# Two-cell recurrence on one core: the sum of the states and the forget products move from GpSimd to VectorE, with a new order of the steps

## The chip, the cores and the metric

The kernel runs on one core of a Trainium2 chip. The metric is the device time in microseconds of one launch, the median of several runs. All times below are microseconds unless marked ns.

A core has engines with a queue each, and each works through its queue in order: TensorE (PE in the profile: matmuls and transposes; its weight loads are listed as PEld), VectorE (DVE), ScalarE (ACT), GpSimd (POOL) and SyncE (SP, which here only issues DMAs). An instruction waits at the head of its queue until the semaphores that it names are high enough; everything behind it on that engine waits with it.

## What is computed

The input is one image of 256 x 256 positions with 32 channels. Four residual layers follow each other, each on the group norm of its input:

```python
x = x + gated_values(gn(x))      # layer 0
x = x + sobel(gn(x))             # layer 1
x = x + sobel(gn(x))             # layer 2
x = x + recurrence(gn(x))        # layer 3
```

The last one takes most of the time. It treats the 256 rows of the image as 256 sequences and the 256 columns as time steps; two cells (layers 0 and 1 of the recurrence) with 128 hidden values each are stacked:

```python
def step(carry, x_t):
    z = x_t @ W_lat + b_lat
    for j in range(2):
        zz = concatenate([z, h[j]]) @ W_cell[j] + b_cell[j]
        zz = group_norm(zz)                    # 4 groups: the 4 gates
        i, f, o, g = split(zz, 4)
        c[j] = sigmoid(f) * c[j] + sigmoid(i) * tanh(g)
        h[j] = sigmoid(o) * tanh(c[j])
        z = z + h[j]
    return x_t + z @ W_out + b_out
```

So a step of a cell needs its own state of the step before, cell 1 needs cell 0's new state too, and the output of a step needs the sum of both states, h[0] + h[1].

## The kernel before, in words

The first three layers take about 640. The recurrence (`recurrence`, from L720) keeps the image in SBUF. The 256 sequences are two halves of 128, one per partition. A step has four units, (layer, half): 00, 01, 10, 11. All of them go through the same operations, each named by a short word in the code:

- x: the product of the input with the folded input weights, for two units at once (`project`, L770); it begins the accumulation of a unit's 128x512 pre-activations `zz` in PSUM. i (L790): for cell 1, the product of cell 0's new state. m (L795): the product of the unit's own state of the step before; it closes `zz`. All three on TensorE.
- sq (L803): the squares of `zz`, on ScalarE. rd (L808): their sums per gate, `ve`, on VectorE. pw (L811): these to the power -0.5, `rs`, 128x4, on GpSimd. The means are zero because the weights were centred beforehand.
- si, sf, so, tg (L784): the four gates, on ScalarE, scaled by `rs`. The output gate has a tile of its own, `go`; the others share `ga`.
- ig (L832): input gate times candidate, VectorE. fc (L837): forget gate times old cell state; on GpSimd for cell 0, on VectorE for cell 1. c (L841): their sum, VectorE. th (L845): its tanh, ScalarE. h (L848): output gate times that, VectorE.
- T (L853): the transpose of h on TensorE into PSUM. e (L857): its copy to SBUF, `hT`, on VectorE; the matmuls i and m of what follows use it as weights.
- hs (`both`, L862): once a step the sum of both cells' `hT`, 128x256, on GpSimd.
- Once in four steps the output of a block of four columns (`emit`): o0 (L868) a matmul of the residual, o1 (L871) four matmuls on the four `hs`, of (L880) the bias on ScalarE, ot a transpose on VectorE and four DMAs on SP.

Nothing is left to a scheduler here. The order on each engine is written out by hand: the table `PLAN` gives each operation of each unit a time within a step of length `PERIOD`, `OUT` does it for the output, and the program adds t x PERIOD, sorts all entries of all 256 steps by that time and issues them in this order. The numbers thus only set the order; an instruction starts when its engine is free and its semaphores are met. Since a unit's operations spread over several periods, several steps are in flight: while cell 0 is at step t, cell 1 is some two steps behind, and `hs` follows later still.

`sums` and `roots` (the tiles of `ve` and `rs`) are rings with one slot for each of the last `SLOTS` steps. A slot that is used again waits for those that used it last.

The kernel has a second copy of the recurrence for norm weights that are not all one and zero; with these inputs it isn't run.

Of the kernel before, what the change touches and what calls it, by code (L numbers as in the profile page):

```python
# [17 lines left out]
T = 256  # L18
# [5 lines left out]
L = 2  # L24
# [633 lines left out]
class RecurrentInputs:  # L658
# [40 lines left out]

SLOTS = 64
PERIOD = 8.700
PLAN = {
    (0, 0): dict(m=3.34, sq=3.72, rd=4.73, pw=5.61, ga=5.84, sf=5.86, so=6.12, fc=6.24),
    (0, 1): dict(m=7.00, sq=7.12, rd=8.38, pw=8.64, ga=9.88, sf=9.90, si=10.02, tg=10.28),
    (1, 0): dict(x=13.81, i=17.21, m=17.59, sq=18.47, rd=19.23, pw=19.73, ga=21.35, sf=21.37),
    (1, 1): dict(x=20.62, i=21.50, m=22.38, sq=23.14, rd=24.02, pw=25.15, ga=25.26, sf=25.28),
}
PLAN[0, 0].update(tg=6.37, si=6.75, ig=7.38, c=8.01, th=8.26, h=8.76, T=9.02, e=10.40)  # L710
PLAN[0, 1].update(fc=10.65, so=11.16, ig=11.28, c=11.54, th=12.17, h=12.55, T=12.92, e=15.19)
PLAN[1, 0].update(so=21.75, si=22.00, tg=22.25, fc=22.63, ig=22.76, c=22.88, th=23.39, h=24.27)
PLAN[1, 0].update(T=24.90, e=25.03)
PLAN[1, 1].update(tg=26.54, si=26.67, so=26.79, ig=26.92, fc=27.05, c=27.55, th=28.31, h=28.81)
PLAN[1, 1].update(T=29.69, e=30.58, hs=34.23)

OUT = dict(o0=29.06, o1=54.28, of=55.29, ot=68.15)


def recurrence(tc, out, ident, weights, inputs, general):  # L720

    nc = tc.nc
# [22 lines left out]
    kp = ctx.enter_context(tc.tile_pool(name="norm", bufs=1))  # L745
    sums = kp.tile([P, 2 * L, SLOTS, 4], F32, name="ve")
    roots = kp.tile([P, 2 * L, SLOTS, 4], F32, name="rs")
    sp = ctx.enter_context(tc.tile_pool(name="state", bufs=2))
# [8 lines left out]
    v = {}  # L757
    todo = []

    def at(when, what, *args):  # L760
        todo.append((when, len(todo), what, args))

    def project(l, h, t):

        if t >= T:
            return
        zz = v["zz", l, h] = ps_zz.tile([P, 4 * H], F32, name=f"zz{l}{h}")
        rows = slice(l * X1, l * X1 + KX)
        x = inputs.of(t, rows, slice(h * P, (h + 1) * P))
        nc.tensor.matmul(zz, lhsT=x, rhs=fx[rows, l, :], start=True, stop=l == 0 and t == 0)  # L770

    def one(name, l, h, t):
        seqs = slice(h * P, (h + 1) * P)
        get = lambda k: v[k, l, h]
        gates = lambda x, g: x[:, g * H : (g + 1) * H]
        four = lambda x: x.rearrange("p (g m) -> p g m", g=4)

        def gate(g, func):

            x, scale = (get("zn"), 1.0) if general else (get("zz"), get("rs")[:, g : g + 1])  # L780
            if g == 2:
                v["go", l, h] = up.tile([P, H], F32, name="go", bufs=3)
            dst = get("go") if g == 2 else gates(get("ga"), g)
            nc.scalar.activation(dst, gates(x, g), func, scale=scale)  # L784

        if name == "x":
            project(0, 1 - h, t + 1 + h)
            project(1, h, t)
        elif name == "i":
            nc.tensor.matmul(  # L790
                get("zz"), lhsT=v["hT", 0, t][:, seqs], rhs=wc[:, l, 0, :], start=False, stop=t == 0
            )
        elif name == "m":
            if t:
                nc.tensor.matmul(  # L795
                    get("zz"),
                    lhsT=v["hT", l, t - 1][:, seqs],
                    rhs=wc[:, l, 1, :],
                    start=False,
                    stop=True,  # L800
                )
        elif name == "sq":
            nc.scalar.activation(  # L803
                sqs[l, h][:, :, 0:H], four(get("zz")), AF.Square, scale=float(H**-0.5)
            )
        elif name == "rd":
            ve = v["ve", l, h] = sums[:, 2 * l + h, t % SLOTS, :]
            nc.vector.tensor_reduce(ve, sqs[l, h], AX.X, ALU.add)  # L808
        elif name == "pw":
            rs = v["rs", l, h] = roots[:, 2 * l + h, t % SLOTS, :]  # L810
            nc.gpsimd.tensor_tensor(rs, get("ve"), inputs.mhalf, ALU.pow)  # L811
        elif name == "ga":
            v["ga", l, h] = up.tile([P, 4 * H], F32, name="ga")
            if not general:
                return
            zn = v["zn", l, h] = up.tile([P, 4 * H], F32, name="zn")
            for g in range(4):
                nc.vector.scalar_tensor_tensor(
                    gates(zn, g),
                    gates(get("zz"), g),  # L820
                    get("rs")[:, g : g + 1],
                    gates(gam[:, l, :], g),
                    ALU.mult,
                    ALU.mult,
                )
            nc.vector.tensor_add(zn, zn, bet[:, l, :])
        elif name in ("si", "sf", "so", "tg"):
            g = ("si", "sf", "so", "tg").index(name)
            gate(g, AF.Tanh if name == "tg" else AF.Sigmoid)
        elif name == "ig":  # L830
            c = v["cn", l, h] = sp.tile([P, H], F32, name=f"c{l}{h}")
            nc.vector.tensor_mul(c, gates(get("ga"), 0), gates(get("ga"), 3))  # L832
        elif name == "fc":
            if t:
                fc = v["fc", l, h] = up.tile([P, H], F32, name="fc")
                eng = nc.vector if l else nc.gpsimd
                eng.tensor_mul(fc, gates(get("ga"), 1), get("c"))  # L837
        elif name == "c":
            c = get("cn")
            if t:  # L840
                nc.vector.tensor_add(c, c, get("fc"))  # L841
            v["c", l, h] = c
        elif name == "th":
            th = v["th", l, h] = up.tile([P, H], F32, name="th")
            nc.scalar.activation(th, get("c"), AF.Tanh)  # L845
        elif name == "h":
            hh = v["h", l, h] = up.tile([P, H], F32, name="h")
            nc.vector.tensor_mul(hh, get("go"), get("th"))  # L848
        elif name == "hs":
            both(t)  # L850
        elif name == "T":
            pt = v["pt", l, h] = ps_h.tile([P, 4 * H], F32, name="pt")
            nc.tensor.transpose(pt[:, 0:P], get("h"), ident)  # L853
        elif name == "e":
            if h == 0:
                v["hT", l, t] = hp.tile([P, S], F32, name=f"hT{l}")
            nc.vector.tensor_copy(v["hT", l, t][:, seqs], get("pt")[:, 0:P])  # L857

    def both(t):

        hs = v["hs", t] = hp.tile([P, S], F32, name="hs")
        nc.gpsimd.tensor_add(hs, *[v.pop(("hT", l, t)) if l else v["hT", l, t] for l in range(L)])  # L862

    def emit(blk, part):

# [24 lines left out]
    for k in range(inputs.NX, NB // inputs.XT):  # L890
        at(((k - inputs.NX + 1) * inputs.XT * J + 2.0) * PERIOD, inputs.load, k)
    for h in range(2):
        at(-1e5, project, 0, h, 0)
    at(PLAN[1, 1]["x"] - PERIOD, project, 0, 0, 1)
    for t in range(T):
        for (l, h), ops in PLAN.items():
            for name, when in ops.items():
                at(t * PERIOD + when, one, name, l, h, t)
    for blk in range(NB):
        for part, when in OUT.items():  # L900
            at((blk * J + J - 1) * PERIOD + when, emit, blk, part)
    todo.sort(key=lambda e: e[:2])
# [45 lines left out]
```

## Time and profile before

| | |
|---|---|
| time, median of 3 runs | 2883.52 (2879.49 to 2886.28) |
| the profiled execution's own time | 2880.13 |
| its span | 2878.2 |
| mean granted TensorE clock | 0.982 |
| TensorE busy | 2776.8 (96%) |
| VectorE busy | 2401.1 (83%) |
| ScalarE busy | 2369.6 (82%) |
| GpSimd busy | 1722.2 (60%) |
| `hs` on GpSimd, 256 times, mean | 774 ns |
| `fc` on GpSimd, 510 times, mean | 455 ns |
| first and last start of `hs` | 669.5, 2868.4 |

The span runs from the first to the last instruction of the profiled execution; its time is a little longer. The busy time of an engine counts neither its waits nor the instructions that only steer. In a line for a group of instructions stand the source line, the engine, the operation, output and inputs with shapes, the count, then the busy time in total and the mean of one in ns, then the idle time of the engine ahead of them and what ended most of it. The chain of waits follows the work that ended last back to its start: a stretch that belongs to TensorE is one in which only faster or better fed TensorE work would help.

### The profile page before, as it was taken

To read this page: it belongs to the slowest core of one execution; us is meant where nothing else is said; L and a number is where in the kernel's file an instruction comes from. 1 tells how busy PE (TensorE), PEld (TensorE's weight loads), DVE (VectorE), ACT (ScalarE), POOL (GpSimd) and SP (SyncE) were. 2 spreads that over 40 slices of the span, in tenths; PEclk is the share of its full clock that TensorE was granted. 3 is DMA by queue.
4 is the path that set the end of the run, shared out by engine and by line. 5 is a ranking of instruction groups with operands and counts; after the bars stand their busy time and mean duration, and the time that the engine had idled before them with its cause. 6 is when DMAs were issued, how large, how long until landed. Compare 5 with 4: busy or idle time off the path is not lost.

```text
span 2878.2 us, 38258 instructions
## 1 busy us (share of the span) xinstructions
PE 2776.8 (96%) x9561; PEld 1034.1 (36%) x9561; DVE 2401.1 (83%) x6505; ACT 2369.6 (82%) x6961; POOL 1722.2 (60%) x2076
## 2 busy tenths in 40 slices
PE   7899898989999999999999999999999999999997
PEld 4433333333333333333333333333333333333332
DVE  6788797977888888888888888888888888888886
ACT  5477676758888888888888888888888888888886
POOL 2311374656666666666666666666666666666665
PEclk9899998989999999999999999999999999999999
DMA  3000000000000000000000000000000000000000
GB/s 133 1 1 1 16 1 1 1 22 8 12 12 12 13 13 12 12 12 11 12 12 12 12 12 12 12 13 15 12 14 13 13 12 12 13 12 12 5 4 9
DMA packets 94333, 38.37 MB, mean 13 GB/s; under 512 B 74852, under 2 KB 91269, under 8 KB 94104
## 3 DMA queue, kind: packets, MB, share of 16 engines
q1 hardware_dynamic: 93156, 34.67, 5.1%
q8 instruction: 81, 1.33, 0.2%
q14 instruction: 148, 1.21, 0.1%
q10 hardware_dynamic: 148, 0.86, 0.1%
q0 software_dynamic: 800, 0.30, 0.0%
HBM read 10.63 MB, written 8.39 MB: 7 GB/s over the span
## 4 chain that ended last, share of the span: by engine, by line
PE 76%; DVE 9%; POOL 7%; ACT 5%; issue 1%; DVEq 0%; POOLq 0%; ACTq 0%
PE zz L795 26%; PE zz L770 15%; PE zz L790 11%; PE pt L853 5%; POOL rs L811 4%; PE pv L279 4%; PE pg L452 4%; DVE c L841 4%; PE pg L412 3%; DVE ve L808 3%; ACT sq L803 3%; PE pg L303 2%; POOL fc L837 2%; ACT ga L784 1%; PE px L871 1%; PE pg L279 1%
## 5 line engine op out<-in xcount | busy, mean ns | idle before, releaser
L811 POOL TENSOR_TENSOR rs<-ve,mhalf 128x4 f32<-128x4 f32 x1024 | 1040.6, 1016 | 539.6 <-DVE ve L808 539.5
L795 PE MATMUL zz<-wc,hT 128*128 128x512 f32 x2040 | 1102.3, 622 | 0.0
L784 ACT ACTIVATE ga<-zz,rs 128x128 f32<-128x128 f32 x3072 | 986.5, 368 | 29.1 <-POOL rs L811 9.9
L808 DVE TENSOR_REDUCE ve<-sq 128x4 f32<-128x516 f32 x1024 | 703.0, 687 | 52.1 <-ACT sq L803 37.2
L803 ACT ACTIVATE sq<-zz 128x512 f32<-128x512 f32 x1024 | 610.2, 596 | 150.9 <-PE zz L795 142.7
L770 PE MATMUL zz<-fx,xt 33*128 33x512 f32 x2048 | 591.7, 643 | 0.8 <-ACT fx L642 0.8
L790 PE MATMUL zz<-wc,hT 128*128 128x512 f32 x1024 | 524.5, 594 | 0.0
L795 PEld LDWEIGHTS zz<-wc,hT 128*128 128x128 f32 x2040 | 324.5, 188 | 555.6 <-DVE hT L857 399.0
L832 DVE TENSOR_TENSOR c<-ga 128x128 f32<-128x128 f32 x1024 | 299.4, 292 | 167.4 <-ACT ga L784 72.3
L845 ACT ACTIVATE th<-c 128x128 f32<-128x128 f32 x1024 | 316.0, 309 | 100.8 <-DVE c L841 100.7
L848 DVE TENSOR_TENSOR h<-go,th 128x128 f32<-128x128 f32 x1024 | 309.5, 302 | 96.9 <-ACT th L845 96.9
L784 ACT ACTIVATE go<-zz,rs 128x128 f32<-128x128 f32 x1024 | 378.8, 370 | 0.0
L837 POOL TENSOR_TENSOR fc<-ga,c 128x128 f32<-128x128 f32 x510 | 232.2, 455 | 244.0 <-ACT ga L784 244.0
L841 DVE TENSOR_TENSOR c<-c,fc 128x128 f32<-128x128 f32 x1020 | 361.6, 355 | 18.4 <-DVE hT L857 0.5
L853 PEld LDWEIGHTS pt<-ident,h 128*128 128x128 f32 x1024 | 142.8, 139 | 542.8 <-DVE h L848 542.3
L853 PE MATMUL pt<-ident,h 128*128 128x128 f32 x1024 | 294.3, 287 | 36.3 <-DVE h L848 36.2
L857 DVE COPY hT<-pt 128x128 f32<-128x128 f32 x1024 | 293.2, 286 | 10.2 <-PE pt L853 2.7
L770 PEld LDWEIGHTS zz<-fx,xt 33*128 33x128 f32 x2048 | 162.2, 185 | 260.6 <-ACT ga L784 193.2
L862 POOL TENSOR_TENSOR hs<-hT,hT 128x256 f32<-128x256 f32 x256 | 198.1, 774 | 2.5 <-DVE hT L857 2.5
L297 DVE TENSOR_TENSOR o<-pv,sg 128x512 f32<-128x512 f32 x256 | 158.1, 681 | 45.8 <-PE pg L279 37.7
L790 PEld LDWEIGHTS zz<-wc,hT 128*128 128x128 f32 x1024 | 162.4, 198 | 68.2 <-issue 56.4
L294 ACT ACTIVATE sg<-pg 128x512 f32<-128x512 f32 x256 | 138.6, 599 | 31.0 <-PE pg L279 25.0
(140 smaller groups left out, 2313.4 us busy)
## 6 DMA issues: line engine op xcount, KB each, us to landing
xt<-xa SPq DMA_DIRECT2D x256, 64.0 KB, 2.0
nat<-in_x_dram SPq DMA_DIRECT2D x16, 512.0 KB, 6.7
out_dram<-st SPq DMA_DIRECT2D x256, 32.0 KB, 1.7
wc<-in_L_conv_W_cell_dram SPq DMA_DIRECT2D x2, 512.0 KB, 4.6
kt<-in_consts_dram ACTq DMA_DIRECT2D x1, 832.0 KB, 5.8
wv<-in_L_conv_Wv_dram POOLq DMA_DIRECT2D x4, 32.0 KB, 4.1
wg<-in_L_conv_Wg_dram POOLq DMA_DIRECT2D x4, 32.0 KB, 5.5
gamma<-in_L_conv_ln_gamma_dram POOLq DMA_DIRECT2D x4, 0.1 KB, 5.9
```

Of the source, the lines that this page charges most:

```text
L770: nc.tensor.matmul(zz, lhsT=x, rhs=fx[rows, l, :], start=True, stop=l == 0 and t == 0)
L784: nc.scalar.activation(dst, gates(x, g), func, scale=scale)
L790: nc.tensor.matmul(get("zz"), lhsT=v["hT", 0, t][:, seqs], rhs=wc[:, l, 0, :], start=False, stop=t == 0)
L795: nc.tensor.matmul(get("zz"), lhsT=v["hT", l, t - 1][:, seqs], rhs=wc[:, l, 1, :], start=False, stop=True,)
L803: nc.scalar.activation(sqs[l, h][:, :, 0:H], four(get("zz")), AF.Square, scale=float(H**-0.5))
L808: nc.vector.tensor_reduce(ve, sqs[l, h], AX.X, ALU.add)
L811: nc.gpsimd.tensor_tensor(rs, get("ve"), inputs.mhalf, ALU.pow)
L832: nc.vector.tensor_mul(c, gates(get("ga"), 0), gates(get("ga"), 3))
L841: nc.vector.tensor_add(c, c, get("fc"))
L845: nc.scalar.activation(th, get("c"), AF.Tanh)
L848: nc.vector.tensor_mul(hh, get("go"), get("th"))
L853: nc.tensor.transpose(pt[:, 0:P], get("h"), ident)
```

## The change

The sum `hs` of the two cells' states and the product `fc` of cell 0 are issued on VectorE; `fc` of cell 1 was there already. GpSimd is left with the powers. `SLOTS` goes from 64 to 32, and `PLAN`, `PERIOD` and `OUT` have new numbers, so the order of the operations changes on VectorE and on ScalarE and the output of a block comes fewer steps after its last state. No operation is added or left out.

```diff
-SLOTS = 64
-PERIOD = 8.700
+SLOTS = 32
+PERIOD = 8.400
 PLAN = {
-    (0, 0): dict(m=3.34, sq=3.72, rd=4.73, pw=5.61, ga=5.84, sf=5.86, so=6.12, fc=6.24),
-    (0, 1): dict(m=7.00, sq=7.12, rd=8.38, pw=8.64, ga=9.88, sf=9.90, si=10.02, tg=10.28),
-    (1, 0): dict(x=13.81, i=17.21, m=17.59, sq=18.47, rd=19.23, pw=19.73, ga=21.35, sf=21.37),
-    (1, 1): dict(x=20.62, i=21.50, m=22.38, sq=23.14, rd=24.02, pw=25.15, ga=25.26, sf=25.28),
+    (0, 0): dict(m=0.30, sq=0.67, rd=1.52, pw=2.74, ga=3.45, sf=3.47, tg=3.83, si=3.96),
+    (0, 1): dict(m=3.59, sq=4.81, rd=5.05, pw=5.78, ga=7.10, si=7.12, tg=7.37, sf=7.49),
+    (1, 0): dict(x=10.53, i=13.70, m=14.79, sq=14.91, rd=15.64, pw=17.23, ga=17.57, sf=17.59),
+    (1, 1): dict(x=16.62, i=18.20, m=18.81, sq=19.78, rd=20.15, pw=21.37, ga=21.95, si=21.97),
 }
-PLAN[0, 0].update(tg=6.37, si=6.75, ig=7.38, c=8.01, th=8.26, h=8.76, T=9.02, e=10.40)
-PLAN[0, 1].update(fc=10.65, so=11.16, ig=11.28, c=11.54, th=12.17, h=12.55, T=12.92, e=15.19)
-PLAN[1, 0].update(so=21.75, si=22.00, tg=22.25, fc=22.63, ig=22.76, c=22.88, th=23.39, h=24.27)
-PLAN[1, 0].update(T=24.90, e=25.03)
-PLAN[1, 1].update(tg=26.54, si=26.67, so=26.79, ig=26.92, fc=27.05, c=27.55, th=28.31, h=28.81)
-PLAN[1, 1].update(T=29.69, e=30.58, hs=34.23)
-
-OUT = dict(o0=29.06, o1=54.28, of=55.29, ot=68.15)
+PLAN[0, 0].update(so=4.20, ig=4.32, fc=4.44, c=4.93, th=5.42, h=5.90, T=6.63, e=6.76)
+PLAN[0, 1].update(ig=7.61, fc=7.85, so=8.10, c=8.46, th=8.58, h=9.56, T=10.29, e=10.65)
+PLAN[1, 0].update(tg=17.83, si=18.44, so=18.57, fc=19.17, ig=19.30, c=19.90, th=20.03, h=20.51)
+PLAN[1, 0].update(T=20.88, e=21.49)
+PLAN[1, 1].update(sf=22.34, tg=22.46, ig=22.83, fc=22.95, so=23.07, c=23.80, th=24.77, h=25.14)
+PLAN[1, 1].update(T=25.75, e=26.48, hs=34.51)
+
+OUT = dict(o0=24.53, o1=40.48, of=44.62, ot=44.86)
...
                 fc = v["fc", l, h] = up.tile([P, H], F32, name="fc")
-                eng = nc.vector if l else nc.gpsimd
-                eng.tensor_mul(fc, gates(get("ga"), 1), get("c"))
+                nc.vector.tensor_mul(fc, gates(get("ga"), 1), get("c"))
...
         hs = v["hs", t] = hp.tile([P, S], F32, name="hs")
-        nc.gpsimd.tensor_add(hs, *[v.pop(("hT", l, t)) if l else v["hT", l, t] for l in range(L)])
+        nc.vector.tensor_add(hs, *[v.pop(("hT", l, t)) if l else v["hT", l, t] for l in range(L)])
```

Sorted within one period, TensorE has m00, T11, i11, T01, m11, x10, m01, T10, i10, m10, T00, x11 after the change. VectorE has rd00, e01, fc10, ig10, c10, rd11, h10, ig00, fc00, e10, c00, rd01, h00, ig11, fc11, e00, c11, rd10, ig01, fc01, h11, c01, hs, h01, e11; ScalarE has sq00, sf10, tg10, si10, so10, sq11, th10, sf00, tg00, si00, so00, sq01, si11, th00, sf11, tg11, so11, sq10, si01, tg01, sf01, th11, so01, th01. Here the first digit is the layer, the second the half.

## The prediction, on record before the result

> **What bounds the kernel now.** I read the busy times first, then the chain of waits, then one disturbed step in the timeline. From the page: TensorE is busy in almost the whole span, and the summed chain lies on it; GpSimd's sum `hs` and product `fc` are much dearer there than VectorE's own products, and `c` on VectorE has a mean (355) above its usual 0.28.
>
> ```profile
> PE 2776.8 (96%) x9561; PEld 1034.1 (36%) x9561; DVE 2401.1 (83%) x6505; ACT 2369.6 (82%) x6961; POOL 1722.2 (60%) x2076
> PE 76%; DVE 9%; POOL 7%; ACT 5%; issue 1%; DVEq 0%; POOLq 0%; ACTq 0%
> L837 POOL TENSOR_TENSOR fc<-ga,c 128x128 f32<-128x128 f32 x510 | 232.2, 455 | 244.0 <-ACT ga L784 244.0
> L841 DVE TENSOR_TENSOR c<-c,fc 128x128 f32<-128x128 f32 x1020 | 361.6, 355 | 18.4 <-DVE hT L857 0.5
> L862 POOL TENSOR_TENSOR hs<-hT,hT 128x256 f32<-128x256 f32 x256 | 198.1, 774 | 2.5 <-DVE hT L857 2.5
> ```
>
> The timeline (start, duration, engine, operation) of two steps shows the same pair of instructions with two outcomes:
>
> ```profile
> 1508.32 0.28 DVE L841 TENSOR_TENSOR c<-c,fc 128x128 f32<-128x128 f32 x1
> 1508.36 0.83 POOL L862 TENSOR_TENSOR hs<-hT,hT 128x256 f32<-128x256 f32 x1
> ...
> 1516.95 0.72 POOL L862 TENSOR_TENSOR hs<-hT,hT 128x256 f32<-128x256 f32 x1
> 1517.00 0.83 DVE L841 TENSOR_TENSOR c<-c,fc 128x128 f32<-128x128 f32 x1
> 1517.45 1.02 PE L795 MATMUL zz<-wc,hT 128*128 128x512 f32 x2
> 1518.68 0.33 PE L853 MATMUL pt<-ident,h 128*128 128x128 f32 x1 [0.21 <-DVE h L848]
> ```
>
> Where `c` starts first it takes 0.28; where `hs` starts 0.05 before it, `c` takes 0.83, the difference 0.55. The chain of waits (start, length) follows what that does: `fc` holds back the power, `hs` holds `c` (cell 0, half 0), then `rd`, `h` and the transpose that TensorE waits for.
>
> ```profile
> 1515.51 0.46 POOL fc L837
> 1515.97 0.00 issue
> 1515.97 1.02 POOL rs L811
> 1516.99 0.01 issue
> 1517.00 0.83 DVE c L841
> 1517.83 0.60 DVE ve L808
> 1518.43 0.21 DVE h L848
> 1518.64 0.04 issue
> 1518.68 0.33 PE pt L853
> ```
>
> The matmul of L795 to the transpose is 1517.45 to 1518.68 = 1.23 here; undisturbed (1500.51 to 1501.37) it is 0.86. TensorE loses 0.37.
>
> **Steady step and TensorE's floor.** `hs` is issued once a step; its starts in the timeline are 1500.10, 1508.36, 1516.95, 1525.93, 1534.70: four steps in 34.60, 8.65 each (all 256: 669.5 to 2868.4, mean 8.62, shorter at the ends). The floor is the sum of the smallest spacings, start to start, in TensorE's timeline. Names: m is the matmul on the layer's own state, i on the state of the layer below, x the pair on the input, T a transpose; two digits are layer and half. m10 to T00 0.86; T00 to x11 0.20; x11 to m00 1.06; m00 to T11 0.96; T11 to i11 0.11; i11 to T01 0.86; T01 to m11 0.11; m11 to x10 0.95; x10 to m01 1.06; m01 to T10 0.96; T10 to i10 0.11; i10 to m10 0.86: 8.10. The two output groups come between a T00 and an x11, one in every second step: 0.78 (1509.63 to 1510.41) and 0.70 in place of 0.20, so 1.08 in four steps, 0.27 a step. Floor 8.37; TensorE stands for 8.65 - 8.37 = 0.28 a step. 0.37 in every second step is 0.19 of it; 0.09 is small change at the other T's and weights.
>
> **What the Trainium skill says.** "SBUF — State Buffer", section "Who interferes with whom": a VectorE instruction with two SBUF inputs contends with a GpSimd instruction that reads SBUF, and whoever issues first blocks the other for its whole instruction. The 0.28 and 0.83 above agree for `hs`. They do not for the power: the one at 1501.14 (1.02) ran through `c` products at 1501.34 and 1501.55 that took 0.29. "Perfetto Trace Analysis", section "Per-instruction lifecycle: what the profiler-reported window actually captures": semaphore waits lie outside the reported window; so I count start to start.
>
> **The change, part by part**, by start-to-start spacing.
> - `hs` leaves GpSimd: the 0.55 on `c00` and with it the 0.37 at T00 go: 0.19 a step. On VectorE the trace has no 128x256 sum. Estimate: 128 columns take 0.29 and space 0.21 (1501.34 to 1501.55), `rd` with 516 columns 0.69: 1.02 ns a column, so 0.34. From below it can't be under 0.21, from above 0.42 with nothing overlapped. It stands between c01 and h01, which waits for th01 (0.32 + 0.34 = 0.66 after c01) anyway: c01's 0.21 and 0.34 fit in the 0.66. Cost 0; uncovered, 0.34 on T01. It sums a step whose transposes were copied a step earlier, so it waits for nothing.
> - Two `fc` of layer 0 leave GpSimd (0.455 each, and the power behind them): two on VectorE at 0.21 spacing (the L837 row of VectorE). fc00 follows ig00 and stands ahead of e10, which comes about 0.4 later; hidden. fc01 is ahead of h11, so 0.21 on that path.
> - VectorE's total: 4 rd at 0.61 (2.44), 20 products, sums and copies at 0.21 (4.20), hs 0.34, output transpose about 0.09, four dependent sums at +0.11 (0.44): 7.5 of 8.37. It doesn't bind by its sum. ScalarE keeps its instructions (30.54 busy in 34.70, 7.6 a step).
> - GpSimd keeps four powers, 4.1 a step, each starting when `ve` is there. pw10 no longer stands behind fc01.
> - New waits: `rd` now waits for GpSimd besides ScalarE (slot used 32 steps before, so always met). The trace shows such second waits on `c` as a sequencer entry of 0.021 on VectorE. An h at 1503.31 and the `c` at 1503.52 behind such an entry are 0.21 apart, as without one: lower bound 0. As upper bound I take 0.08, four times the entry, as an estimate; for the sum 0.03. `c` of layer 0 loses such a wait. The 64 to 32 slots change nothing else.
> - The order. On TensorE the cyclic order is the same, the outputs still between T00 and x11. On VectorE e01 goes ahead of fc10, c11 behind e00; on ScalarE th10 goes ahead of sf00 and the gates of a cell change places. Input loads keep their place in steps; a block's output, with its four DMAs on SP, comes 2.5 steps sooner (68.15/8.70 = 7.8 steps, then 44.86/8.40 = 5.3), and nothing on TensorE waits for it.
>
> **Does something else become late?** Latencies, start to start, where the consumer stood waiting: m to sq 1.11 (1.16 behind x), sq to rd 0.61, rd to pw 0.77, pw to first gate 1.04, gate to product 0.40, product to sum 0.32, sum to th 0.32, th to h 0.34, h to T 0.33, T to e 0.32, last gate to x 0.45; ScalarE's spacing is 0.25 a gate, 0.48 a sq, 0.20 a th. Put m00 at 0; TensorE unhindered has T11 at 0.96, m01 4.05, T10 5.01, m10 5.98, T00 6.84, x11 7.04.
> - Cell 00: sq 1.16, rd 1.77, pw 2.54; ScalarE is at sq11 and th10 until 3.83; gates 3.83 to 4.58; ig 4.73, fc 4.94, e10 5.33, c 5.54; th00 5.94 behind si11; h00 6.28, but rd01 holds VectorE until 6.44; T00 can go at 6.77, wanted at 6.84: slack 0.07.
> - Cell 01: sq 5.21, rd 5.82, pw 6.59, si 7.63, tg 7.88, sf 8.13, th11 8.38; h11 8.74 behind fc01; T11 at 9.07, wanted at 9.06: late by 0.01. c01 8.95, th01 9.27, hs until 9.50, h01 9.61, e11 9.82, m11 at about 10.17, wanted at 10.14: late by 0.03.
> - x11 needs so11: 6.64 + 0.45 = 7.09, wanted at 7.04: late by 0.05.
> So about 0.05 to 0.08 in a step without output, nothing in a step with one (TensorE is 0.5 later there): 0.03 to 0.04 a step. With 0.03 per rd, 8.37 + 0.04 = 8.41.
>
> **Sum.** 8.65 - 8.41 = 0.24 over some 253 steps (the ends of the pipeline aside) = 61. The stages ahead (the first transpose of the recurrence is at 643.8) and the tail are unaltered. Against its own execution: 2880.13 (span 2878.2, 1.9 around it) - 61 = 2819; the median is 3.4 above that execution, so 2822.
>
> **Rivals.**
> 1. Tight slack is missed. Cell 01's path to T11 has none left; for it speaks that gates, th11 and fc01 stand in one chain. If it and T00 come 0.3 late, every step without output loses 0.3, 0.15 a step: 8.52, gain 33, 2850. Against: the latencies are those of waiting consumers.
> 2. Only the 0.19 goes and the small change of 0.09 stays: 8.46, gain 48, 2835. I count it with the likeliest.
> 3. Slower: VectorE now runs 17 instructions with two SBUF inputs a step, not 14, and if each held off the powers by the lock, a power starts late. A power late by 0.3 makes no loss yet (rival 1); it decides at 0.28 a step on average: at 0.55 late, steps without output lose 0.55 and those with one 0.01. At 0.6 late the loss is (0.60 + 0.06)/2 = 0.33, the step 8.70: 13 over the 2883.5, 2896. For: the skill's sentence. Against: the power's 1.007 to 1.03 in the midst of such products.
>
> **How the numbers follow.** Likeliest (with 2) 0.74, own range from the floor 8.37 (gain 71, 2812, less 4 for the spread of runs: 2808) to 8.48 (2840). Rival 1 0.18, rival 3 0.05, and 0.03 for no effect, if TensorE finds other waits for all of it. 2808 to 2853 leaves out rival 3, no effect and the upper part of rival 1. 0.2% is 5.8 us, about what a measurement can tell. Faster 0.92, same 0.02, slower 0.06.
>
> **What would show it.** `c` of L840 at 0.29 with none at 0.83; GpSimd with 1024 powers alone; `hs` on VectorE near 0.42 and T01 not later for it; steps near 8.41; L795 to the transpose 0.86 to 0.96 nearly everywhere. Wrong if T11 or T00 waits 0.3 for h, if rd starts over 0.7 after sq, if powers lengthen.

## The result and the profile after

| | before | after |
|---|---|---|
| time, median | 2883.22 | 2843.14 |
| ratio, 95% interval | | 0.9863 (0.9847 to 0.9878) |
| profiled execution, span | 2880.13, 2878.2 | 2843.08, 2841.3 |
| steady step, from one start of T00 to the next, four in a row | 9.05, 8.97, 8.32, 8.26 | 8.61, 8.32, 8.75, 8.32 |
| its mean, T00 of step 50 to T00 of step 230 | 8.653 | 8.511 |

The change gains 40, forecast were 61. The time lies in the range on record, the gain is two thirds of the forecast. 0.142 less in a step over 256 steps is 36, and the two profiled spans differ by 37; the profiled execution of the kernel before is 3 faster than the median. The longer steps are those with an output, which follows the T00 that begins the step: before, two steps in a row and then two without (the prediction has them as every second step; the mean is the same), after, every second step.

The page of the changed kernel, in the same lines as before: busy time of each engine, and the chain that ended last.

```profile
PE 2765.1 (97%) x9561; PEld 1029.8 (36%) x9561; DVE 2493.5 (88%) x7271; ACT 2361.1 (83%) x6961; POOL 1310.0 (46%) x1310
...
PE 94%; DVE 2%; POOL 1%; ACT 1%; issue 0%; DVEq 0%; POOLq 0%; ACTq 0%
...
L840 DVE TENSOR_TENSOR c<-c,fc 128x128 f32<-128x128 f32 x1020 | 287.8, 282 | 6.8
```

`c` now has the mean 282 ns (355 before), and 9% of VectorE and 7% of GpSimd on the chain have become 2% and 1%. The timeline shows `hs` behind `c01`, and the transpose T00 0.87 behind the start of the matmul m10 (1502.72 to 1503.59), where before it was 1.23 in the steps with an output. The fourth line is the first matmul of the output, which follows T00:

```profile
1502.72 1.02 PE L795 MATMUL zz<-wc,hT 128*128 128x512 f32 x2
...
1503.25 0.28 DVE L847 TENSOR_TENSOR h<-go,th 128x128 f32<-128x128 f32 x1
...
1503.59 0.33 PE L852 MATMUL pt<-ident,h 128*128 128x128 f32 x1
...
1503.76 0.60 PE L867 MATMUL px<-xa,e 128*128 128x256 f32 x2
...
1505.78 0.28 DVE L840 TENSOR_TENSOR c<-c,fc 128x128 f32<-128x128 f32 x1
...
1505.99 0.41 DVE L861 TENSOR_TENSOR hs<-hT,hT 128x256 f32<-128x256 f32 x1
```

So the wait that the forecast named is gone. What came in its place? The trace has the first answer. The first two lines below are rd's instructions and the entries that only wait, which stand in the queue ahead of them (DVEq); then follow one rd early and one later in the run, each with its sq.

```profile
L808 DVE TENSOR_REDUCE ve<-sq x1024: 673/691/693, 638.8 to 2826.7; 128x4 f32<-128x516 f32 x171
L808 DVEq EVENT_SEMAPHORE  x900: 21/21/50, 638.7 to 2826.7; - x180
```

```profile
822.05 0.60 ACT L803 ACTIVATE sq<-zz 128x512 f32<-128x512 f32 x1 [0.29 <-PE zz L795]
...
822.68 0.69 DVE L808 TENSOR_REDUCE ve<-sq 128x4 f32<-128x516 f32 x1
```

```profile
1501.95 0.60 ACT L803 ACTIVATE sq<-zz 128x512 f32<-128x512 f32 x1 [0.26 <-PE zz L795]
...
1502.65 0.69 DVE L808 TENSOR_REDUCE ve<-sq 128x4 f32<-128x516 f32 x1
```

From the start of sq to the start of rd it is 0.63 at 822 and 0.70 at 1502. The break is sharp: 0.61 to 0.63 up to step 31, 0.68 to 0.70 from step 32 on (19 of these 896 rd, at 0.75 to 1.05, aside), which is where the ring of 32 slots is used again and rd gets its second wait, on GpSimd. The step changes with it: the mean of steps 6 to 30 is 8.432, later it is 8.511; a step without output goes from 8.25 to 8.32. 900 rd have an entry, which takes 0.021: 896 are the four rd in each of the 224 steps from step 32 on, and four come before the ring is used again.

### The profile page after: what moved, and what is told of

Its sections match the earlier page's. It is cut to its first block, busy times and chain, and to the rows that moved or that the text cites. A ratio compares the mean times of both kernels' runs of the same rounds, so it can differ in the third digit from the quotient of the medians.

```text
span 2841.3 us, 38649 instructions
## 1 busy us (share of the span) xinstructions
PE 2765.1 (97%) x9561; PEld 1029.8 (36%) x9561; DVE 2493.5 (88%) x7271; ACT 2361.1 (83%) x6961; POOL 1310.0 (46%) x1310
## 4 chain that ended last, share of the span: by engine, by line
PE 94%; DVE 2%; POOL 1%; ACT 1%; issue 0%; DVEq 0%; POOLq 0%; ACTq 0%
PE zz L795 34%; PE zz L770 19%; PE zz L790 15%; PE pt L852 5%; PE pv L279 4%; PE pg L452 4%; PE pg L412 3%; PE pg L303 2%; PE px L870 1%; PE pg L279 1%; PE pc L238 1%; PE px L867 1%; POOL xb L262 1%; PE pg L422 0%; DVE ve L808 0%
## 5 line engine op out<-in xcount | busy, mean ns | idle before, releaser
L784 ACT ACTIVATE ga<-zz,rs 128x128 f32<-128x128 f32 x3072 | 924.7, 366 | 30.0 <-POOL rs L811 11.0
L784 ACT ACTIVATE go<-zz,rs 128x128 f32<-128x128 f32 x1024 | 389.3, 380 | 0.0
L847 DVE TENSOR_TENSOR h<-go,th 128x128 f32<-128x128 f32 x1024 | 291.7, 285 | 11.9 <-ACT th L844 1.5
L836 DVE TENSOR_TENSOR fc<-ga,c 128x128 f32<-128x128 f32 x1020 | 297.0, 291 | 0.6 <-ACT ga L784 0.6
L840 DVE TENSOR_TENSOR c<-c,fc 128x128 f32<-128x128 f32 x1020 | 287.8, 282 | 6.8
L279 PE MATMUL pv<-xb,wv 32*128 32x512 f32 x512 | 158.0, 629 | 0.0
```

What stands on the lines that cost most here:

```text
L279: nc.tensor.matmul(ps, lhsT=w[rows, half * P : (half + 1) * P], rhs=mn, start=True, stop=True)
L836: nc.vector.tensor_mul(fc, gates(get("ga"), 1), get("c"))
```

## The experiments

Steps in the table are mean distances of T00's starts from step 50 to 230 in each run's trace. Each ratio is to runs of the kernel before that were taken beside it (medians 2881.4 to 2884.1). Times in a unit's path are counted from T00. In kernels with the edit of the first experiment, line numbers are 4 higher.

| kernel | order | `hs` on | `fc` of cell 0 on | step | median | ratio to before, 95% |
|---|---|---|---|---|---|---|
| before | old | GpSimd | GpSimd | 8.653 | 2883 | |
| after | new | VectorE | VectorE | 8.511 | 2843.1 | 0.9863 (0.9847, 0.9878) |
| mirror | new | VectorE | VectorE | 8.436 | 2826.2 | 0.9796 (0.9780, 0.9812) |
| hs_only | old | VectorE | GpSimd | 8.744 | 2904.6 | 1.0071 (1.0054, 1.0088) |
| fc_only | old | GpSimd | VectorE | 8.982 | 2967.8 | 1.0290 (1.0273, 1.0307) |
| both_old | old | VectorE | VectorE | 9.271 | 3041.7 | 1.0548 (1.0531, 1.0566) |
| old_fixed | old, two entries moved | VectorE | VectorE | 8.439 | 2829.9 | 0.9825 (0.9808, 0.9841) |
| order_only | new | GpSimd | GpSimd | 8.563 | 2858.3 | 0.9917 (0.9900, 0.9933) |
| hs_back | new | GpSimd | VectorE | 8.654 | 2883.2 | 0.9998 (0.9990, 1.0007) |
| th_first | new, th11 earlier | VectorE | VectorE | 8.495 | 2842.7 | 0.9862 (0.9845, 0.9878) |
| best | new, th11, e11, `hs` moved | VectorE | VectorE | 8.458 | 2833.1 | 0.9831 (0.9815, 0.9848) |
| hs_late | new, e11, `hs` moved | VectorE | VectorE | 8.437 | 2827.7 | 0.9806 (0.9790, 0.9823) |

All but before, after, hs_only and order_only walk the ring as mirror does.

### The second wait of rd

```diff
+    def slot(t):
+        turn, k = divmod(t, SLOTS)
+        return SLOTS - 1 - k if turn % 2 else k
...
-            ve = v["ve", l, h] = sums[:, 2 * l + h, t % SLOTS, :]
+            ve = v["ve", l, h] = sums[:, 2 * l + h, slot(t), :]
...
-            rs = v["rs", l, h] = roots[:, 2 * l + h, t % SLOTS, :]
+            rs = v["rs", l, h] = roots[:, 2 * l + h, slot(t), :]
```

Where the ring is walked back and forth, the first slot used again in a pass is the one used last. The wait for it covers all other slots of the pass, and rd needs a second wait in one step of 32 only.

> The changed kernel with the ring of slots walked forwards and backwards in turn, so that one wait in 32 steps covers all slots of the last pass; nothing else differs. Theory (the second wait of rd is what makes the step 8.50 where 8.41 was forecast): sq to rd falls from 0.70 to 0.63 in all steps, and the step from 8.51 to 8.43, as in the first 32 steps of the changed kernel's own trace: 224 x 0.07 = 16 us less, 2827. Rival (the shorter steps at the start are an effect of the filling pipeline): 2843, steps stay at 8.51 after the 32nd.

The same group of rd in mirror:

```profile
L812 DVE TENSOR_REDUCE ve<-sq x1024: 690/691/693, 638.8 to 2810.2; 128x4 f32<-128x516 f32 x171
L812 DVEq EVENT_SEMAPHORE  x32: 21/21/50, 638.7 to 2550.1; - x32
```

32 entries where there were 900, sq to rd 0.61 to 0.63 (and 0.70 in the one step of 32 that still has the entry), steps of 8.26, 8.54, 8.26, 8.68, and 2826.2. That is 17 less than the changed kernel; 0.075 x 224 steps is 17. The theory stands: the second wait makes each rd start 0.07 later.

The entry is not the new wait. By the semaphores in the trace of the changed kernel, the entry holds the wait for ScalarE, and rd itself the one for GpSimd. So the entry ends its wait 0.63 after the start of sq, just when rd starts in mirror, and rd follows 0.064 behind the entry.

The rd that TensorE feels is rd01, which stands ahead of h00 and so of T00. In mirror T00 is 0.39 behind h00 (1498.19 to 1498.58), and the next matmul 0.11 behind T00; in the changed kernel it is 0.34 and 0.17 (1503.25, 1503.59, 1503.76 above). Of some 0.07 in a usual step, 0.055 is thus the matmul that follows T00 later when T00 only just has its `h`, and the rest is a wait of T00 itself. The few rd that start later still make up the 0.075; mirror has none of them, and what delays them is not shown.

```profile
1498.19 0.28 DVE L851 TENSOR_TENSOR h<-go,th 128x128 f32<-128x128 f32 x1
...
1498.58 0.27 PE L856 MATMUL pt<-ident,h 128*128 128x128 f32 x1
...
1498.69 0.60 PE L871 MATMUL px<-xa,e 128*128 128x256 f32 x2
```

### The moves without the order

hs_only is the second of these edits to the kernel before, fc_only the first, both_old has both; the old order stays.

```diff
-                eng = nc.vector if l else nc.gpsimd
+                eng = nc.vector
...
-        nc.gpsimd.tensor_add(hs, *[v.pop(("hT", l, t)) if l else v["hT", l, t] for l in range(L)])
+        nc.vector.tensor_add(hs, *[v.pop(("hT", l, t)) if l else v["hT", l, t] for l in range(L)])
```

> The kernel before with hs alone on VectorE, old order, fc of cell 0 still on GpSimd. Theory (the lock costs 0.55 in half of the steps, and the sum in VectorE's queue between c00 and rd01 costs 0.34 in all of them): nearly nothing is won, step 8.58 to 8.66, 2865 to 2885. Rival (the lock's 0.19 a step comes back whole): 8.46, 2835.

> The kernel before with fc of cell 0 on VectorE, hs still on GpSimd, old order (ring walked back and forth). Theory (hs on GpSimd is the main cost): c00 still takes 0.83 in a good part of the steps; what is won is pw10's 0.46 behind fc01: step 8.55 to 8.65, 2855 to 2882. Rival (fc on GpSimd was the cost): 2840 or less.

> The kernel before, in its own order of steps, with hs and both fc on VectorE (ring walked back and forth, so that rd gets no second wait). Theory (the order was needed: in the old one hs stands between c00 and rd01, 0.34 on the way to T00): c never 0.83 any more, but c00 to rd01 0.55 in each step where it was 0.31 and 0.75 in turn; pw10 is freed of fc01; step 8.50 to 8.62, 2845 to 2875. Rival (the new order is worth nothing): 2827, as the changed kernel without the second wait.

All three are slower than before, and slower than either theory had it. In hs_only all `c` are at 0.28 to 0.29, so the lock (a VectorE instruction held by one of GpSimd, or the other way round) is gone from c00. But `hs` stands between c00 and rd01, and the power behind that rd01 takes 1.19 where 1.01 is usual:

```profile
1503.48 0.28 DVE L841 TENSOR_TENSOR c<-c,fc 128x128 f32<-128x128 f32 x1
...
1503.68 0.42 DVE L862 TENSOR_TENSOR hs<-hT,hT 128x256 f32<-128x256 f32 x1
...
1504.01 0.68 DVE L808 TENSOR_REDUCE ve<-sq 128x4 f32<-128x516 f32 x1
...
1504.78 1.19 POOL L811 TENSOR_TENSOR rs<-ve,mhalf 128x4 f32<-128x4 f32 x1 [1.32 <-DVE ve L808]
...
1505.99 0.88 ACT L784 ACTIVATE ga<-zz,rs 128x128 f32<-128x128 f32 x3 [0.41 <-POOL rs L811]
```

c00 to rd01 is 0.53 in every step, where before it was 0.31 in steps without output and 0.75 in those with one. pw01 takes 1.19 in nearly every step of hs_only and both_old; there ig11 starts 0.04 after it and fc11 0.20 behind ig11, both on VectorE with two inputs from SBUF. The gates of unit 01 wait for it (last line; before, ScalarE hardly ever waited for a power), and T11 comes 0.20 later in steps without output. By these two together those steps are 0.36 longer (8.66, before 8.30), those with an output 0.18 shorter (8.83, before 9.01), and the mean grows by 0.09. No run has that `hs` without the longer pw01, so what each costs is not shown apart.

In fc_only c00 takes 0.28 too, against the expectation: `hs` starts 0.12 behind it. In fc_only and both_old the main cause is another that I hadn't seen. The timeline of both_old:

```profile
1503.38 0.60 ACT L807 ACTIVATE sq<-zz 128x512 f32<-128x512 f32 x1 [0.31 <-PE zz L799]
...
1504.28 0.29 DVE L841 TENSOR_TENSOR fc<-ga,c 128x128 f32<-128x128 f32 x1 [0.56 <-ACT ga L788]
...
1504.49 0.28 DVE L861 COPY hT<-pt 128x128 f32<-128x128 f32 x1
...
1504.69 0.68 DVE L812 TENSOR_REDUCE ve<-sq 128x4 f32<-128x516 f32 x1
...
1504.83 1.12 PE L799 MATMUL zz<-wc,hT 128*128 128x512 f32 x2 [0.42 <-DVE hT L861]
```

fc00 stands at the head of VectorE's queue and waits 0.56 for its forget gate, which ScalarE gives late since sq11 and others go first. Behind it stand e01 and rd11, whose input is ready: sq to rd of unit 11 is 1.31 here (mean 1.36) in place of 0.63, and TensorE waits 0.42 for e01 (last line). On GpSimd the same wait delayed pw11 alone, by 0.02 in the mean. In both_old `hs` stands between c00 and rd01 besides, as in hs_only. To see whether these two places, of fc00 and of `hs`, are all of it, old_fixed moves two numbers of the old plan:

```diff
-    (0, 0): dict(m=3.34, sq=3.72, rd=4.73, pw=5.61, ga=5.84, sf=5.86, so=6.12, fc=6.24),
+    (0, 0): dict(m=3.34, sq=3.72, rd=4.73, pw=5.61, ga=5.84, sf=5.86, so=6.12, fc=7.45),
...
-PLAN[1, 1].update(T=29.69, e=30.58, hs=34.23)
+PLAN[1, 1].update(T=29.69, e=30.58, hs=37.70)
```

> As both_old, but fc00 behind ig00 and hs behind c01, in the old order otherwise. Theory (what made both_old slow is fc00, which waited for its gate in front of e01 and rd11, and hs in front of rd01): sq to rd of unit 11 falls from 1.36 back to 0.63, step 8.43 to 8.52, 2825 to 2850. Rival (the old order as a whole can't carry the products on VectorE): over 2900.

2829.9, with the step at 8.439, and pw01 takes 1.01: the 212 between both_old and old_fixed are these two entries. The old order with both of them placed well does what the new order does (mirror 8.436). The rest of the new order, PERIOD among it, is worth nothing that these runs show.

### The order without the moves

order_only has both of these edits to the changed kernel, hs_back the second alone.

```diff
-                nc.vector.tensor_mul(fc, gates(get("ga"), 1), get("c"))
+                eng = nc.vector if l else nc.gpsimd
+                eng.tensor_mul(fc, gates(get("ga"), 1), get("c"))
...
-        nc.vector.tensor_add(hs, *[v.pop(("hT", l, t)) if l else v["hT", l, t] for l in range(L)])
+        nc.gpsimd.tensor_add(hs, *[v.pop(("hT", l, t)) if l else v["hT", l, t] for l in range(L)])
```

> The changed kernel's order with hs and fc of cell 0 back on GpSimd (SLOTS 32; rd has no second wait here, since c waits for GpSimd anyway). Theory (the order was made for the placement): fc01 holds pw10 back by about 0.6 in each step, hs on GpSimd stands against VectorE's products of two SBUF inputs; step 8.6 to 8.8, 2870 to 2920, no faster than before. Rival (the order alone brings the gain): 2845 or less.

> mirror with hs alone back on GpSimd, new order. Theory (after the runs so far: the lock costs only where the other engine's two-input work falls at the same time; in the new order hs on GpSimd falls on rd00, which has one input): hs costs nothing there, and its move was worth nothing beside the order: step 8.42 to 8.45, 2822 to 2831. Rival (hs on GpSimd costs wherever it stands): over 2840, with an e, h or c of 0.5 and more.

Both went against the theory. order_only is 23 faster than the runs of the kernel before beside it. fc01 does hold pw10 back (rd to pw of unit 10 is 1.39, 0.62 more), but the gates of unit 10 stand behind sq00 on ScalarE in any case (free at 2.90 + 0.48 = 3.38 after T00; pw10 allows them at 2.26 + 1.04 = 3.30). And `hs`, pushed behind pw10, comes to lie on rd00, whose one input from SBUF isn't disturbed (third and fourth line); so c00's 0.83 is gone by order alone. The steps with an output, where it was, go from 9.01 to 8.63, by 0.37 as the forecast had it; those without grow from 8.30 to 8.49. What stays is fc01 against h11 (first two), and fc00 against h10 (0.44 in the mean):

```profile
1504.29 0.46 POOL L837 TENSOR_TENSOR fc<-ga,c 128x128 f32<-128x128 f32 x1 [1.06 <-ACT ga L784]
...
1504.38 0.51 DVE L848 TENSOR_TENSOR h<-go,th 128x128 f32<-128x128 f32 x1
...
1505.73 0.72 POOL L862 TENSOR_TENSOR hs<-hT,hT 128x256 f32<-128x256 f32 x1
...
1505.96 0.69 DVE L808 TENSOR_REDUCE ve<-sq 128x4 f32<-128x516 f32 x1
```

In hs_back fc01 is off GpSimd, so pw10 is punctual, and `hs` follows it 0.7 sooner: just ahead of h01.

```profile
1503.85 0.73 POOL L865 TENSOR_TENSOR hs<-hT,hT 128x256 f32<-128x256 f32 x1
...
1504.05 0.67 DVE L851 TENSOR_TENSOR h<-go,th 128x128 f32<-128x128 f32 x1 [0.38 <-ACT th L848]
```

h01 takes 0.67 in nearly every step, 0.38 more than its 0.29; e11 and rd00 stand behind it (sq to rd of unit 00 is 0.81), and all that the order had won is lost. So `hs` on GpSimd is dear or free by what happens to run on VectorE beside it. The one-line difference between hs_back and mirror is 57.

The four steps from before to after, in one order of making them, by the medians of the table: new order 25 less, `fc` to VectorE 25 more, `hs` to VectorE 57 less, rd's second wait 17 more. In another order of making them the single numbers would differ; both_old shows how much.

### What sets the steps without output

mirror has 8.26 in a step without output, the floor is 8.10. The forecast put T11 behind the path sq01, rd01, pw01, gates, th11, h11. th_first takes th11 ahead of sf01 on ScalarE, and h11 ahead of fc01 (first edit below); hs_late takes `hs` behind c10 and e11 ahead of h01 (second edit); best, so named before it ran, has both edits.

```diff
-PLAN[1, 1].update(sf=22.34, tg=22.46, ig=22.83, fc=22.95, so=23.07, c=23.80, th=24.77, h=25.14)
+PLAN[1, 1].update(sf=22.34, tg=22.46, ig=22.83, fc=22.95, so=23.07, c=23.80, th=24.23, h=24.60)
...
-PLAN[1, 1].update(T=25.75, e=26.48, hs=34.51)
+PLAN[1, 1].update(T=25.75, e=26.20, hs=28.40)
```

> mirror with th11 ahead of sf01 on ScalarE and h11 ahead of fc01 on VectorE. Theory (steps without output are set by the path sq01, rd01, pw01, gates, th11, fc01, h11, T11): T11 gets its h 0.27 sooner, its wait goes; c01 and h01 come 0.1 later and T01 or m11 takes over a part: step from 8.43 to 8.39-8.43, 2815 to 2826. Rival (that path isn't what binds): 2826 or more.

> mirror with hs behind c10 and e11 ahead of h01, ScalarE's order as it was. Theory (hs does stand in the way of e11, which m11 waits for: m11 comes 0.05 late in steps without output): step 8.40 to 8.43, 2815 to 2824. Rival (hs and e11 where they are cost nothing, T11 alone sets the step): 2825 to 2828.

> th_first, and hs behind c10 instead of c01, e11 ahead of h01, ring walked back and forth. Theory: with h11 early, e11 and h01 no longer stand behind hs; T11, T01 and m11 all come without a wait; step 8.37 to 8.40, 2808 to 2818. Rival (T00 behind rd01 or the weight loads bind next): 2820 to 2826.

None is faster than mirror. In th_first h11 comes at 1.68 after T00, not 1.94, and T11 no longer waits; but sf01 stands behind th11 now, so fc01, c01, th01 and h01 are 0.1 to 0.2 later, e11 stands behind h01 (3.13, was 3.02), and m11, which needs e11, loses more than T11 gained: steps without output are 8.37. In best e11 is no longer behind h01; the steps without output are 8.30 and 8.27 in turn, since T01 waits for h01 in the first (0.35 behind it). In hs_late e11 is at 2.64 to 2.70 and m11 free, yet the step is mirror's: what m11 wins in one step (8.22), rd11 behind `hs` loses in the step in which the output's transpose is on VectorE too (8.71, in mirror 8.68; sq to rd of unit 11 is 0.95 there, 0.63 in mirror). So T11, T01 and m11 hang on the same stretch of ScalarE and VectorE, and these edits only hand the wait on. Whether another order gets nearer to the floor stays open.

mirror is the fastest run here, 2826.2; the intervals of hs_late and old_fixed overlap with its own.

## Why the prediction was right or wrong

- **The lock on c00 as TensorE's loss of 0.19 a step: right, in place and size.** c00's 0.83 and T00's 1.23 are gone, and where the order alone takes them away, a step with an output is 0.37 shorter (order_only). That the move was needed for it was too simple: the order alone gets rid of it as well (order_only), and the moves without the order make matters worse (both_old).
- **`hs` on VectorE at no cost in its place: right.** It takes 0.418 (estimate 0.42), c01 to h01 is 0.66 with it, as without, and taking it elsewhere wins nothing (hs_late).
- **fc00 hidden, fc01 0.21 on h11's path: right for this order**, and h11's path couldn't be relieved of it for a gain (th_first). What fc00 costs in a place where its gate is late (fc_only is 84 slower than before) the forecast didn't ask: it looked at what is queued behind the new instructions in the new order only.
- **The new wait of rd: wrong in size, and this is the step that failed.** I took 0.03 with the bounds 0 and 0.08, and let at most 0.01 of it (3 in all) into the step. It is 0.07 a rd and 0.075 a step: 17, so 14 of the 21 that were missing. The slack of 0.07 that the forecast gave T00 was about right (mirror has 0.05), but rd01 took more than all of it, and a T00 that just has its `h` costs another 0.055 at the matmul behind it, which the forecast's sum doesn't have. The line I went by, an h at 1503.31 and a `c` at 1503.52 with an entry between, was another case: that entry waited for VectorE's own earlier work and was through while VectorE was still busy. rd stands at the head of the queue, its entry holds the late wait, the one for ScalarE, and there the entry counts. At 0.68 to 0.70 rd stays just under the forecast's own sign of being wrong, over 0.7.
- **Slack at T11, T00 and m11: the places right, the sum too small.** Forecast were 0.05 to 0.08 in a step without output; mirror, without the second wait, has 0.16. From T00, in mirror and forecast: h11 1.94 and 1.90, T11 2.28 and 2.22 to 2.23, e11 3.02 and 2.98, sq01 6.63 and 6.47. Of the 0.16, 0.05 comes ahead of m00 (at 1.31, unhindered 1.26), where the forecast had x11 late by 0.05; then 0.02 at T11, 0.05 at i11 and 0.04 at m11. The forecast lacked i11's: T11 starts 0.34 behind h11, the usual latency, but the matmul behind it then follows at 0.16 and not at 0.11, as with T00 above. m11's two passes are 0.47 apart and not 0.43. In steps with an output mirror has 8.54 and 8.68; the floor's sum gives 8.60 and 8.68, since its 0.70 was read behind a T00 that was late itself. Over both kinds of steps mirror is 0.07 over the floor, 0.03 more than forecast, 8 in all.
- **14 and 8 are 22**; 21 were missing. That 2843 lies in the range is no merit of these two terms: the range reached to 2853 for the sake of the first rival.
- **Rivals.** The first, cell 01's path to T11 late by 0.3 in steps without output (8.52, 2850), is nearer to the measured step (8.511) than the likeliest (8.41), but no transpose comes 0.3 late: a step without output is at 8.32, 0.22 over the floor, from the small waits above. It had the chance 0.18. The second (8.46) lies between mirror (8.436) and the changed kernel. The third, powers held off by VectorE, is out for this change: they take 1.012 in the mean, 1.016 before, among 17 products and sums of two inputs a step, and rd to pw is 0.77 as before. But VectorE's products seem able to lengthen a power: pw01 takes 1.19 in hs_only and both_old.

## What to carry to other kernels

An instruction that goes to another in-order queue is to be priced by who stands behind it while it waits: the same two moves came out 158 dearer (both_old) or 52 cheaper (old_fixed) than the kernel before, and the difference is two entries in an order. Before GpSimd is given work that reads SBUF, look which instructions of VectorE with two SBUF inputs will run beside it. And where a buffer ring makes an instruction wait on a second engine for something long done, walk the ring back and forth or let a wait that is there anyway cover it.

## What the runs showed of the hardware

- An rd that waits at the head of VectorE's queue for ScalarE starts 0.07 later if it has a wait on GpSimd too, long met: 0.63 and 0.70 from sq to rd, with a queue entry of 0.021 in the trace that holds the wait for ScalarE. A `c` behind a busy VectorE, whose entry was through ahead of time, showed none of it.
- A GpSimd sum or product of two SBUF inputs lengthens a VectorE sum or product of two SBUF inputs that starts after it (0.28 to 0.83 and 0.29 to 0.67 beside `hs`, 0.28 to 0.51 beside `fc`); it doesn't lengthen rd, which has one (0.69). A power of 128x4 on GpSimd lengthened none, though it takes 1.01 and reads SBUF: the sums and products that start during one take 0.31 at most. The Trainium skill, "SBUF — State Buffer", section "Who interferes with whom", has any VectorE instruction with two SBUF inputs contend with any GpSimd instruction that reads SBUF; for a VectorE instruction that starts during a power no run here shows that, and the measurement decides. That the first to issue keeps the ports for its whole instruction the section says of VectorE's two-port modes; the prediction took it for all.
- The power itself takes 1.18 to 1.19 and not 1.01 where a VectorE product of two SBUF inputs starts 0.03 to 0.04 after it and the next one 0.201 to 0.204 behind that: nearly every step of hs_only and both_old, some of best. With the next one 0.208 to 0.25 behind, it takes 1.00 to 1.02 in all runs. Why is not shown.
- A transpose that starts 0.33 behind its `h`, about the least seen, is followed by the matmul of i or o0 at 0.16 to 0.17; one that starts 0.35 to 0.36 behind it, at 0.14 to 0.15; from 0.38 on, at 0.11 to 0.12.
- GpSimd's own `hs` takes 0.72 if it starts first and 0.83 if a `c` started 0.04 ahead of it.
